# Routing of a mixture of experts, taken apart and placed among the maxima of the first batch

## The chip, the cores and the metric

The kernel runs on one core of a Trainium2 chip. A core has five engines with a queue of instructions each: TensorE (PE in the profile; its weight loads are listed apart as PEld), VectorE (DVE), ScalarE (ACT), GpSimd (POOL) and SyncE (SP, which here only issues DMAs). They run beside each other and wait for each other through semaphores. Each works its own queue off in order. Products of TensorE land in PSUM, everything else lies in SBUF, and DMAs move data between SBUF and the memory outside (DRAM).

The metric is the device time of the whole program in microseconds. Lower is better.

## What is computed

Two layers over `x` of shape (4, 2048, 256), each an attention `s` and a gate `g`, joined as `x + s * silu(g)`. Layer 0 has a windowed attention and an FP8 linear layer. Layer 1, to which the change belongs, has a causal attention with 16 heads of 16 and rotary positions, and a mixture of 8 experts of which each token takes two:

```python
x = x + s0 * silu(ffn0)            # layer 0, on layernorm(x)
xn = layernorm(x)
q, k = rope(xn @ wq.T + bq), rope(xn @ wk.T + bk);  v = xn @ wv.T + bv
att = softmax(where(causal, q @ k.T * 0.25, -inf))
s = (att @ v) @ wo.T + bo
# experts
scores = softmax(xn @ wg);  gates, idx = top_k(scores, 2);  gates /= gates.sum(-1)
m = one_hot(idx) laid out as (2 * T, 8), all first choices before all second ones
loc = ((cumsum(m, 0) - 1) * m).sum(-1)          # place of a choice in its expert
valid = loc < cap;   disp[idx, min(loc, cap - 1)] += xn * valid
out = relu(disp @ w1 + b1) @ w2 + b2
g = sum over the two choices of gates * valid * out[idx, loc]
x = x + s * silu(g)
```

Here T is 8192 tokens and `cap` is 2048, so there are 16384 choices and 16384 slots.

## The kernel before

**Stages.** Layer 0 runs over 16 segments of 512 tokens, in a software pipeline whose steps are written out in a dictionary (`plan`). It also leaves layer 1's normalised rows in DRAM (`xn_d`), their transposes (`xT_d`), the values (`va_d`) and the logits of the experts' choice in SBUF, and it projects q and k of batch 0 (`project`), which go to `qk_d`. Then comes the routing, alone. Then, for each of the four batches, the *maxima* (the largest score of each row and head, over the causal part) and the *attention* (exponentials of the scores less that maximum, and their products with the values). The expert networks are a generator, `experts`, whose pieces are put among the maxima and the attentions of the first three batches and the maxima of the fourth; beside attention `b` the q and k of batch `b + 1` are projected. The last attention has the output projection and the joining of the layers (`finish`) beside it.

**Order.** On TensorE, VectorE, ScalarE and GpSimd the order of the instructions is the order of the program inside `manual_schedule` blocks: layer 0 is one such block, everything from the maxima on is another. What lies between (the routing, L670 to L797, and the first loads) isn't in such a block, and SP's queue isn't ordered by hand either.

**The ring.** `ring` holds four places, each with `qT`, `kT` and `va` of one block of 512 tokens. At the start GpSimd clears all `qT` and sets all `kT` to one (L629, L630), and `fetch` loads a block by four DMAs for q, four for k (128 KB each, L646) and one for the values (L647), all on SP, blocks 0, 1, 2, 3.

**Routing.** `choose` takes the two experts of the last two segments (for the first 14 it has run inside layer 0) into one-hot vectors `oh` and numbers `kmax`. L707 to L726 count the choices ahead of each one: two float32 products with a triangle and with the counts of each partition, masked and summed to `loc`. The rest turns places round: for every slot, which token is in it (`source`). It is a product of two one-hot matrices over 128 columns of choices, in 16 rounds of 8: `at_row` says in which row of a 128 x 128 grid of slots a choice lies, `at_col` in which column, times the token's number plus one. In half of the rounds VectorE makes `at_row` by one comparison (L781), in the others ScalarE by eight squares and one `Relu` (L775, L779). `source` is the list by which GpSimd gathers the experts' rows (L1042).

**Maxima.** `maxima` goes over query blocks `qb` 0 to 3, their four row tiles `r`, four groups of four heads `g`, and the key blocks up to `qb`: 160 score steps a batch. A step is four products into two pair slots of PSUM (`scores`, L830; there are three slots). A full key block is reduced by VectorE straight from PSUM (L898). Of the diagonal one ScalarE copies the square tile out (L902), GpSimd masks it (L912), VectorE reduces the masked tile later (L921) and what lies left of it from PSUM (L905). `whole` (L929) makes the row maximum of all parts; `spread` transposes a block's maxima on TensorE (L937), copies them (L939) and sends them by four DMAs (L941) into spare rows of that block's `qT`, from where the attention's products subtract them. These three are put on a list (`later`) and run some steps on; after the last block seven turns (`TAIL`) empty it.

**Filling.** Before each step `feed` is called with the stall that a planner (`Plan`, with costs of each step) expects on TensorE. It runs pieces of `experts` up to that stall, as long as they aren't 2 us ahead of their share: `IN_M`, 0.209 of all expert work in each batch of maxima, and `IN_A`, 0.055 in each of the first three attentions. In the attention `along` lets the side that is most behind its share step next, and one whose accumulation is open (`held`) before others. The attention goes over query blocks 3, 2, 1, 0.

Of the kernel before, what the change touches and what calls it, by code (L numbers as in the profile page):

```python
# [19 lines left out]
P = 128  # L20
# [24 lines left out]
def d2_kernel(ctx: ExitStack, tc: tile.TileContext, t: dict):  # L45
# [59 lines left out]
    oh = const.tile([P, 2, NT, E], F32, tag="oh", name="oh")  # L105
# [110 lines left out]
    with ExitStack() as l0:  # L216
        w0 = l0.enter_context(tc.tile_pool(name="w0", bufs=1))
        p2 = l0.enter_context(tc.tile_pool(name="l0p2", bufs=2))
        small = l0.enter_context(tc.tile_pool(name="l0small", bufs=4))

# [386 lines left out]
    with tc.tile_pool(name="bvp", bufs=1) as bvp:  # L607
        bvc = bvp.tile([P, 2], F32, tag="bvc", name="bvc")
        nc.scalar.dma_start(out=bvc, in_=t["bv"].rearrange("(c p) -> p c", p=P))
        bvr = bvp.tile([P, 2, P], F32, tag="bvr", name="bvr")  # L610
        nc.scalar.copy(bvr, bc(bvc[:, :, None], [P, 2, P]))
        pb = mm_tile()
        for c in range(2):
            nc.tensor.matmul(
                pb[:, :D], lhsT=bvr[:, c, :], rhs=wo[:, c, :], start=(c == 0), stop=(c == 1)
            )
        nc.vector.tensor_tensor(bo, bo, pb[:, :D], ALU.add)


# [5 lines left out]
    for n in range(NBLK):  # L625
        qT = w1p.tile([P, 4, SEG], F32, tag=f"qT{n}", name=f"qT{n}")
        kT = w1p.tile([P, 4, SEG], F32, tag=f"kT{n}", name=f"kT{n}")
        va = w1p.tile([P, SPT, VW], F32, tag=f"va{n}", name=f"va{n}")
        nc.gpsimd.memset(qT, 0.0)  # L629
        nc.gpsimd.memset(kT, 1.0)  # L630
        ring.append((qT, kT, va))
# [3 lines left out]
    ready = set()  # L635

    def fetch():

        while free and made_qk:
# [3 lines left out]
            for dst, s_ in ((qT, 0), (kT, 1)):  # L643
                src = qk_d[4 * b + i, s_].rearrange("(g j r) n -> j r g n", g=4, j=4)
                for j in range(4):
                    nc.sync.dma_start(out=dst[32 * j : 32 * j + HD, :, :], in_=src[j])  # L646
            nc.sync.dma_start(out=va, in_=va_d[4 * b + i])  # L647
            ready.add((b, i))

    made_qk.extend((0, i) for i in range(4))  # L650
# [21 lines left out]


    with ExitStack() as rt:
        rp = rt.enter_context(tc.tile_pool(name="route", bufs=1))
        KJ = 2 * NT

        def rtile(shape, tag):
            return rp.tile(shape, F32, tag=tag, name=tag)

        tok = rtile([P, NT], "tok")
        nc.gpsimd.iota(
            tok, pattern=[[P, NT]], base=1, channel_multiplier=1,
            allow_small_or_imprecise_dtypes=True,
        )
        along_f = rtile([P, P], "along")
        nc.gpsimd.iota(
            along_f, pattern=[[1, P]], base=0, channel_multiplier=0,
            allow_small_or_imprecise_dtypes=True,
        )  # L690
        ones = rtile([P, P], "ones")
        nc.gpsimd.memset(ones, 1.0)
        tri = rtile([P, P], "tri")
        nc.gpsimd.affine_select(
            out=tri, in_=ones, compare_op=ALU.is_gt, fill=0.0,
            base=0, pattern=[[1, P]], channel_multiplier=-1,
        )

        choose(rp, slice(EARLY * SPT, NT))

        ohf = oh.rearrange("p k t e -> p (k t e)")
        ohj = oh.rearrange("p k t e -> p (k t) e")
        pc = mm_tile()
        for e in range(E):
            nc.tensor.matmul(  # L707
                pc[:, e : e + 1], lhsT=ohj[:, :, e], rhs=ones[:, 0:1], start=True, stop=True
            )
        counts = rtile([P, E], "counts")  # L710
        nc.scalar.copy(counts, pc[:, :E])
        ahead = rtile([P, KJ, E], "ahead")
        nc.vector.tensor_tensor(
# [639 lines left out]
```

## Time and profile before

The three runs shown took 3890.49, 3900.05 and 3896.63 us, a median of 3896.63. The profile is of one execution.

| | us |
|---|---|
| median of three runs | 3896.63 |
| the profiled execution, as timed | 3874.95 |
| its span, first to last instruction | 3873.2 |
| TensorE's last product of layer 0 ends | 482.5 |
| first score of the maxima | 544.2 |
| first expert product | 554.0 |
| batch 0: last score step of blocks 0 and 1 | 663.3 |
| batch 0: first score of the attention | 957.8 |
| first scores of the attention of batches 1, 2, 3 | 1798.6, 2632.2, 3460.2 |

Times inside the profile are from the start of the span. Engines overlap, so busy times don't add up to the span. A releaser (`<-`) is what ended a wait, inferred from semaphores. TensorE's records are modelled at their ends, so a busy TensorE isn't one at its peak. A float32 product appears as two records. The granted clock is a share of full speed.

### The profile page before, as it was taken

What the parts mean: (1) busy time and instruction counts of PE and PEld (TensorE: products, weight loads), DVE (VectorE), ACT (ScalarE), POOL (GpSimd) and SP (SyncE); (2) the same over time, 40 slices, a digit from 0 to 9 for tenths busy, and PEclk for the clock granted to TensorE, in tenths of its full rate; (3) what the DMA queues carried; (4) which work ended last, traced back from release to release, by engine and by line L of the source; (5) the groups of instructions that cost most, each with busy time, mean ns of one, the idle gap of its engine ahead of it and who ended that gap; (6) DMA issues with size and microseconds to landing.
All of it is one profiled execution on the core that took longest, in us unless ns stands there. A gap on an engine that the chain in (4) does not pass through costs nothing.

```text
span 3873.2 us, 53698 instructions
## 1 busy us (share of the span) xinstructions
PE 3672.9 (95%) x21724; PEld 1502.7 (39%) x21724; DVE 2186.5 (56%) x2842; ACT 1773.1 (46%) x2781; POOL 809.4 (21%) x1016
## 2 busy tenths in 40 slices
PE   7999779999999899999999999999999999989998
PEld 3555454444223244443222344443233344433332
DVE  7999768887111258885112278882112478863344
ACT  4665342212666541213666531115666421127775
POOL 4554231110000121110001221110101211013344
PEclk8999889999999999999999999999999999999999
DMA  2444450010120220100022211000112201013232
GB/s 80 143 138 139 167 111 16 30 35 12 33 56 13 75 59 12 46 23 14 31 65 50 58 30 41 16 22 18 53 38 59 53 30 35 12 47 110 89 102 79
DMA packets 131803, 216.86 MB, mean 56 GB/s; under 512 B 18657, under 2 KB 86498, under 8 KB 131554
## 3 DMA queue, kind: packets, MB, share of 16 engines
q1 hardware_dynamic: 116642, 177.21, 15.9%
q0 software_dynamic: 12288, 33.57, 2.9%
q8 instruction: 171, 2.80, 0.3%
q10 hardware_dynamic: 2624, 2.63, 0.2%
q14 instruction: 78, 0.64, 0.1%
HBM read 128.99 MB, written 83.85 MB: 55 GB/s over the span
## 4 chain that ended last, share of the span: by engine, by line
PE 79%; DVE 14%; POOL 2%; DMA 2%; issue 1%; ACT 1%; SPq 0%; POOLq 0%; ACTq 0%; DVEq 0%
PE sp L830 32%; PE so L1006 13%; PE so L1087 13%; PE so L1069 12%; PE so L189 3%; DVE mp L898 3%; DVE rb L203 2%; PE so L955 2%; DVE cm L404 1%; DVE w L406 1%; DVE ra L199 1%; POOL xs L344 1%; POOL xq L346 1%; PE so L1056 1%; DVE mp L921 1%
## 5 line engine op out<-in xcount | busy, mean ns | idle before, releaser
L986 ACT ACTIVATE pt<-sp 128x1024 f32<-128x1024 f32 (+3 forms) x1280 | 1076.6, 893 | 527.2 <-PE sp L830 526.1
L898 DVE TENSOR_REDUCE mp<-sp 128x2 f32<-128x1024 f32 x768 | 904.5, 1220 | 188.3 <-PE sp L830 184.4
L830 PE MATMUL sp<-kT,qT 32*128 32x512 f32 (+3 forms) x5120 | 743.6, 579 | 20.4 <-ACT dg L902 13.1
L830 PE MATMUL sp<-qT,kT 32*128 32x512 f32 (+3 forms) x5120 | 690.8, 583 | 10.0 <-DMA qT<-nT 10.0
L1006 PE MATMUL so<-pt,va 128*32 128x512 f32 (+3 forms) x5120 | 602.7, 543 | 7.5 <-POOL pt L991 6.9
L1087 PE MATMUL so<-w,hT 128*128 128x256 f32 x2048 | 572.5, 404 | 5.2 <-DVE rb L203 4.5
L1069 PE MATMUL so<-xTe,w 128*128 128x512 f32 x1024 | 544.7, 635 | 18.9 <-DVE rb L203 15.2
L902 ACT COPY dg<-sp 128x256 f32<-128x256 f32 x512 | 165.4, 375 | 744.7 <-PE sp L830 712.0
L1087 PEld LDWEIGHTS so<-w,hT 128*128 128x128 f32 x2048 | 350.8, 190 | 358.2 <-issue 312.3
L991 POOL TENSOR_SCALAR_AFFINE_SELECT pt<-pt 128x512 f32<-128x512 f32 x256 | 166.3, 653 | 1236.0 <-ACT pt L986 1130.6
L912 POOL TENSOR_SCALAR_AFFINE_SELECT dg<-dg 128x512 f32<-128x512 f32 x256 | 162.4, 635 | 1249.3 <-ACT dg L902 1243.1
L830 PEld LDWEIGHTS sp<-kT,qT 32*128 32x128 f32 x5120 | 261.6, 185 | 384.0 <-DVE mp L898 142.4
L1075 ACT ACTIVATE hT<-so,b 128x512 f32<-128x512 f32 x256 | 175.9, 687 | 412.9 <-PE so L1069 412.4
L830 PEld LDWEIGHTS sp<-qT,kT 32*128 32x128 f32 x5120 | 225.4, 185 | 291.4 <-issue 203.8
L199 DVE SCALAR_TENSOR_TENSOR ra<-so,bqk,tab 128x512 f32<-128x512 f32 x48 | 36.0, 750 | 480.9 <-PE so L189 480.9
L905 DVE TENSOR_REDUCE mp<-sp 128x2 f32<-128x256 f32 (+2 forms) x384 | 247.4, 687 | 87.7 <-ACT dg L902 86.2
L1069 PEld LDWEIGHTS so<-xTe,w 128*128 128x128 f32 x1024 | 164.8, 190 | 322.2 <-issue 259.3
L1006 PEld LDWEIGHTS so<-pt,va 128*32 128x32 f32 x5120 | 101.4, 108 | 409.5 <-issue 338.2
L1012 DVE STREAM_TRANSPOSE avq<-so 128x512 f32<-128x512 f32 x64 | 45.8, 716 | 365.0 <-PE so L1006 363.4
L921 DVE TENSOR_REDUCE mp<-dg 128x8 f32<-128x1024 f32 x128 | 155.0, 1211 | 28.1 <-POOL dg L912 28.1
L1093 DVE TENSOR_TENSOR ot<-so,b 128x512 f32<-128x512 f32 x64 | 43.7, 683 | 207.2 <-PE so L1087 207.2
L1121 POOL DMA_INDIRECT o<-eout,slot_g x128 | 123.6, 966 | 147.2 <-DVE fz L1149 102.5
(165 smaller groups left out, 2752.4 us busy)
## 6 DMA issues: line engine op xcount, KB each, us to landing
qk_d<-ra SPq DMA_DIRECT2D x128, 128.0 KB
w<-in_w_dram SPq DMA_DIRECT2D x16, 1024.0 KB
eout<-ot SPq DMA_DIRECT2D x32, 512.0 KB
va_d<-vas SPq DMA_DIRECT2D x16, 574.0 KB
va<-va_d SPq DMA_DIRECT2D x16, 574.0 KB
x<-in_x_dram SPq DMA_DIRECT2D x16, 512.0 KB
tab<-in_rope_dram SPq DMA_DIRECT2D x16, 512.0 KB
rec<-rec_d SPq DMA_DIRECT2D x32, 256.0 KB
```

The costliest lines, as they stand in the source:

```text
L830: nc.tensor.matmul(pairs[j // 2][:, j % 2, :w], lhsT=lhsT[r0 : r0 + 32], rhs=rhs[r0 : r0 + 32], start=True, stop=True,)
L898: nc.vector.tensor_reduce(mp[:, h0 : h0 + 2, kc], sp, AX.X, ALU.max)
L902: nc.scalar.copy(dg[:, d0 : d0 + 2, :], sp[:, :, r * P : w])
L905: nc.vector.tensor_reduce(mp[:, h0 : h0 + 2, qb + 1], sp[:, :, : r * P], AX.X, ALU.max)
L912: nc.gpsimd.affine_select(out=dg[:, d0 : d0 + 4, :], in_=dg[:, d0 : d0 + 4, :], compare_op=ALU.is_ge, fill=NEG, base=0, pattern=[[0, 4], [ ...
L921: nc.vector.tensor_reduce(mp[:, 4 * g - 4 : 4 * g + 4, qb], dg, AX.X, ALU.max)
L986: nc.scalar.activation(pt[:, 2 * p : 2 * p + 2, c0:], sp[:, :, : SEG - c0], AF.Exp, scale=SCALE)
L991: nc.gpsimd.affine_select(out=pt[:, :, c0 : c0 + P], in_=pt[:, :, c0 : c0 + P], compare_op=ALU.is_ge, fill=0.0, base=0, pattern=[[0, 4], [ ...
L1006: nc.tensor.matmul(av[32 * j : 32 * j + 32, c0:], lhsT=va[:, kt % 4, h0 : h0 + 32], rhs=pt[:, j, c0:], start=(kt == 0), stop=last,)
L1069: nc.tensor.matmul(ph, lhsT=w1[:, c, hc * P : (hc + 1) * P], rhs=xT[:, c, :], start=(c == 0), stop=(c == 1),)
L1075: nc.scalar.activation(hT[:, hc, :], ph, AF.Relu, bias=b1[:, hc : hc + 1])
L1087: nc.tensor.matmul(po[:, u * D : (u + 1) * D], lhsT=hT[:, hc, a * P : (a + 1) * P], rhs=w2[:, hc, :], start=(hc == 0), stop=(hc == 7),)
```

## The change

It does these things at once:

- The routing becomes a generator, `route`, in the hand-ordered part. `feed` runs one piece of it at each score step of batch 0 as long as there are any, and no expert piece meanwhile. It ends at the 44th call. The next call issues the first gather of the experts, and expert pieces follow when the planner's TensorE time is 8 us further.
- Whole numbers that bfloat16 holds exactly are kept in it: `oh`, the triangle, the counts ahead, `in_e`, `at_col`, `at_row`. A token's number no longer fits, so it is split: `oh1` carries its row plus one, `oh2` its tile, and `at_col` has two halves, one made by VectorE and one by GpSimd. One product of 256 columns makes both sums; `first_` and `src` join them. All sixteen `at_row` are made by ScalarE. `in_e` is made a round at a time.
- The product of `bv` with `wo` that completes `bo` is the routing's last piece.
- Blocks 1 and 0 are loaded first, q on SP's queue, k on ScalarE's, the values after; then blocks 3 and 2 on SP. VectorE clears `qT`, GpSimd still sets `kT`.
- In the maxima the rows of blocks 1 and 0 alternate, then come block 3 and block 2. The last block's `spread` is returned and becomes a piece (`due`) of the attention that follows, or runs ahead of the last attention.
- The list `later` is emptied by as many turns as it needs, with less expert work in each. Batch 0 has a share of 0.186 of the experts, the others 0.216.
- The pools of layer 0 are opened in another order; the row maxima have a pool of their own; `avq` and `yq` have one buffer.

The core of the diff, with unchanged pieces of moved code left out:

```diff
-    oh = const.tile([P, 2, NT, E], F32, tag="oh", name="oh")
+    oh = const.tile([P, 2, NT, E], BF16, tag="oh", name="oh")
...
-        w0 = l0.enter_context(tc.tile_pool(name="w0", bufs=1))
         p2 = l0.enter_context(tc.tile_pool(name="l0p2", bufs=2))
         small = l0.enter_context(tc.tile_pool(name="l0small", bufs=4))
+        w0 = l0.enter_context(tc.tile_pool(name="w0", bufs=1))
...
-        nc.gpsimd.memset(qT, 0.0)
+        nc.vector.memset(qT, 0.0)
...
-    def fetch():
+    def fetch(queues=(nc.sync, nc.sync)):
+        later = []
         while free and made_qk:
...
-            for dst, s_ in ((qT, 0), (kT, 1)):
+            for dst, s_, queue in ((qT, 0, queues[0]), (kT, 1, queues[1])):
...
-                    nc.sync.dma_start(out=dst[32 * j : 32 * j + HD, :, :], in_=src[j])
-            nc.sync.dma_start(out=va, in_=va_d[4 * b + i])
+                    queue.dma_start(out=dst[32 * j : 32 * j + HD, :, :], in_=src[j])
+            later.append((va, va_d[4 * b + i]))
+        for va, src in later:
+            nc.sync.dma_start(out=va, in_=src)
...
-    made_qk.extend((0, i) for i in range(4))
+    made_qk.extend(((0, 1), (0, 0)))
+    fetch((nc.sync, nc.scalar))
+    made_qk.extend(((0, 3), (0, 2)))
     fetch()
...
+    def route(rp):
...
+        choose(rp, slice(EARLY * SPT, NT))
+        plan2.on("DVE", 5.0)
+        yield 0
...
+        oh1 = rtile([P, 2, NT, E], "oh1", BF16)
+        nc.vector.tensor_scalar(oh1, oh, row1, None, ALU.mult)
+        oh2 = rtile([P, 2, NT, E], "oh2", BF16)
+        nc.vector.tensor_tensor(
+            oh2, oh, bc(along_f[:, None, :NT, None], [P, 2, NT, E]), ALU.mult
+        )
...
+        def build(n):
+            js = slice(n * NB, (n + 1) * NB)
+            in_e = rtile([P, NB, CT], "in_e", BF16, 2)
+            nc.vector.tensor_tensor(
+                in_e, bc(along_f[:, None, :CT], [P, NB, CT]),
+                bc(rowcol[:, 1, js, None], [P, NB, CT]), ALU.is_equal,
+            )
+            at_col = rtile([P, NB, 2, P], "at_col", BF16, 2)
+            for i, (engine, o) in enumerate(((nc.vector, oh1), (nc.gpsimd, oh2))):
+                engine.tensor_tensor(
+                    at_col[:, :, i, :].rearrange("p j (e c) -> p j e c", c=CT),
+                    bc(o.rearrange("p k t e -> p (k t) e")[:, js, :, None], [P, NB, E, CT]),
+                    bc(in_e[:, :, None, :], [P, NB, E, CT]), ALU.mult,
+                )
+            plan2.on("DVE", 1.6)
+            at_row = rtile([P, NB, P], "at_row", BF16, 3)
+            for u in range(NB):
+                nc.scalar.activation(
+                    at_row[:, u, :], along_f, AF.Square,
+                    bias=minus_row[:, n * NB + u : n * NB + u + 1],
+                )
+            nc.scalar.activation(at_row, at_row, AF.Relu, scale=-1.0, bias=one)
+            plan2.on("ACT", 3.1)
+            made[n] = at_row, at_col
+
+        for n in range(NJ + 1):
+            if n < NJ:
+                build(n)
+                yield 0
+            if n > 0:
+                at_row, at_col = made.pop(n - 1)
+                for u in range(NB):
+                    j = (n - 1) * NB + u
+                    nc.tensor.matmul(
+                        ps[:, : 2 * P], lhsT=at_row[:, u, :],
+                        rhs=at_col[:, u, :, :].rearrange("p i c -> p (i c)"),
+                        start=(j == 0), stop=(j == KJ - 1),
+                    )
+                yield 0.9
...
-        for qb in range(4):
+        rows_ = [(q, r) for r in range(SPT) for q in (1, 0)]
+        rows_ += [(q, r) for q in (3, 2) for r in range(SPT)]
+        nms, last = {}, None
+        for qb, r in rows_:
...
-            later.append((3, spread))
-        for _ in range(TAIL):
+            if (qb, r) == rows_[-1]:
+                last = spread
+            else:
+                later.append((3, spread))
+        while later:
             turn()
-            feed(2.0, 1.0)
+            feed(1.0, 1.0)
+        return last
...
+    def one_piece(f):
+        f()
+        yield 0.58
...
-    IN_M = (1.0 - (B - 1) * IN_A) / B
+    IN_M = [0.186] + [(1.0 - 0.186 - (B - 1) * IN_A) / (B - 1)] * (B - 1)
...
-            exp.step()
+            began = None
             def feed(us, share):
+                nonlocal began
+                if not rt.over:
+                    rt.step()
+                    return
+                if began is None:
+                    exp.step()
+                    began = plan2.t["PE"]
+                if plan2.t["PE"] < began + 8.0:
+                    return
...
-                    maxima(mp_, b, feed)
+                    if b == 0:
+                        rt = Side(route(rs.enter_context(tc.tile_pool(name="route", bufs=1))), 0.0)
+                    spread = maxima(mp_, b, feed)
+                    rt.drain()
+                due.queue.append(one_piece(spread))
                 if b + 1 == B:
+                    exp.close()
+                    due.drain()
                     break
```

## The prediction

> **What bounds the kernel now.** I read the page first (busy shares, the row of slices), then the busy times by stretch, the chain of waits, the groups of each stretch, and last the timeline at the places that the change touches.
>
> ```profile
> PE 3672.9 (95%) x21724; PEld 1502.7 (39%) x21724; DVE 2186.5 (56%) x2842; ACT 1773.1 (46%) x2781; POOL 809.4 (21%) x1016
> ...
> PE   7999779999999899999999999999999999989998
> ```
>
> TensorE is busy nearly everywhere, so time is TensorE's work plus its idle time, and a change pays by the idle time it removes. The slices hide where that lies; the stretches show it (columns: PE, weight load, DVE, ACT, POOL, each with its count, then clock, DMA share, GB/s):
>
> ```profile
> 482.50:554.00 71.50, 47.43 (x308) 40.64 (x309) 42.91 (x64) 31.74 (x82) 19.61 (x18) 0.80 0.78 146
> 544.00:663.30 119.30, 113.20 (x578) 51.63 (x578) 86.92 (x106) 34.37 (x85) 31.85 (x44) 0.97 0.06 19
> 663.30:957.80 294.50, 287.52 (x1418) 130.01 (x1418) 245.38 (x245) 55.29 (x117) 39.26 (x52) 0.99 0.08 26
> ```
>
> The first is the routing: TensorE's last product of layer 0 ends at 482.5, its first score starts at 544.2, the first expert product at 554.0. The second holds batch 0's maxima of query blocks 0 and 1, the third those of 2 and 3. In both, experts fill TensorE.
>
> **The routing's price, and what replaces it.** The groups between 482 and 544 us (busy, mean ns | idle before):
>
> ```profile
> L766 DVE TENSOR_TENSOR at_col<-ahead,in_e 128x1024 f32<-128x1024 f32 x16 | 19.4, 1222 | 2.6 <-PE mm L787 2.4
> ...
> L775 ACT ACTIVATE at_row<-along,minus_row 128x128 f32<-128x128 f32 x64 | 19.6, 388 | 16.5 <-DVE minus_row L749 10.9 <-PE mm L787 5.5
> L779 ACT ACTIVATE at_row<-at_row,ones 128x1024 f32<-128x1024 f32 x8 | 9.2, 1148 | 0.3
> ...
> L787 PE MATMUL mm<-at_col,at_row 128*128 128x128 f32 x256 | 31.4, 286 | 10.0 <-DVE at_col L766 9.4 <-ACT at_row L779 0.2
> ```
>
> The change deletes this stretch and gives the same work to the 48 score steps of blocks 1 and 0, one piece a step, with no expert before the pieces end (step 44) and 8 us of planned TensorE time more, so until about step 48. What counts is when those 48 steps end. Before, that was at 663.3, with expert work done beside them:
>
> ```profile
> L1069 PE MATMUL so<-xTe,w 128*128 128x512 f32 x64 | 35.1, 645 | 0.2 <-ACT xTe L1059 0.2
> ...
> L1087 PE MATMUL so<-w,hT 128*128 128x256 f32 x110 | 29.6, 398 | 0.0
> ```
>
> A float32 product has two records here and takes 0.95 us (four records in 1.91 of the chain) and 0.48 us: 32 x 0.95 + 55 x 0.48 + 2.2 for transposes = 59 us of experts, about 62 with some 3 us of alternation. They must be done later, at full price. So the new kernel breaks even here if its 48 steps end at 663.3 - 62 = **601 us**.
>
> VectorE's share of the 48 steps, from the same groups: 32 full maxima in pairs of 2.36 us (37.8), 16 diagonal ones of 1.21 (19.4), the left parts 6.0 + 10.3 + 14.6, eight row maxima (1.5): 89.6 us. Routing on VectorE, start to start: choosing 4.2 (483.8 to 488.0), `ahead` 1.1, `spot` 1.3, `loc` 1.1, the casts 0.8, `oh1` and `oh2` 1.5, sixteen blocks of `in_e` (0.2) and `at_col` (1.15) 21.5, the tail 2.3: 33.9 us. ScalarE now makes all sixteen `at_row`: 2.45 + 1.15 = 3.6 us each, 57.6, beside 32 x 0.65 = 20.8 of diagonal copies: 78 us, less than VectorE's 123.5. Per piece pair it is 4.25 against at least 5.1 in block 1, and 4.9 against 4.2 only in row 1 of block 0. TensorE's 128 products shrink below the old 0.24 us each and lie in idle time: no charge, nor would 31 us bind.
>
> When can they start? First places: eight loads of 128 KB for block 1's q and k, then eight for block 0's. The loads of before ran at this rate:
>
> ```profile
> 504.00:508.00 4.00, 0.00 (x0) 0.00 (x0) 3.93 (x12) 1.27 (x5) 0.00 (x0) 0.54 1.09 127
> ```
>
> The DMA engines are full (1.09) at 127 GB/s, 1.05 us a load; a second issuing queue can't add to that. From about 483 (SP is behind the `va_d` store issued at 482.9, ScalarE's queue behind its last copy) q1 and k1 take 8.4 us, with 2 us of landing to 493; the second step also wants k of block 0, 8.4 us later, at 502. If SP takes its loads ahead of that store (`qT`'s clearing moves to VectorE, idle from 475.4), it is 5 us less. I take 500; choosing (4.2) runs before that. VectorE then has 123.5 - 4.2 = 119.3 us: 619 without gaps.
>
> Gaps: three pair slots, two per step. In each of block 1's sixteen head groups the full step needs a slot that the diagonal's left maximum frees, so VectorE waits one score step (1.07) less the second left maximum (0.38 to 0.91), or for a diagonal maximum queued between: 0.5 us each, 8 us. At the clock of a half-idle TensorE (0.50 between 488 and 500) a step takes 1 us more: 24. I take 16, nearer the middle since TensorE will be some 45% busy. The end: **635 us**, 34 late.
>
> [...]
>
> ```profile
> 487.57 1.80 POOL L630 MEMSET kT<- 128x2048 f32 x1
> ...
> 488.02 1.43 DVE L728 TENSOR_SCALAR base<-kmax 128x128 f32<-128x128 f32 x1
> ```
>
> L728 took 1.43 us instead of the 0.23 of its kind and ended just after the memset on POOL. [...]
>
> **The seams.** Before, block 3 is last in the maxima and first in attention:
>
> ```profile
> 954.63 0.23 DVE L929 TENSOR_REDUCE nm<-mp 128x16 f32<-128x80 f32 x1
> 954.92 0.09 PEld L937 LDWEIGHTS so<-ident,nm 128*16 128x16 f32 x1 [2.51 <-DVE nm L929]
> 954.92 0.38 PE L937 MATMUL so<-ident,nm 128*16 128x128 f32 x1 [2.22 <-DVE nm L929]
> ...
> 957.78 0.51 PEld L830 LDWEIGHTS sp<-qT,kT 32*128 32x128 f32 x8 [2.77 <-DMA qT<-nT]
> 957.78 2.09 PE L830 MATMUL sp<-qT,kT 32*128 32x512 f32 x8 [2.47 <-DMA qT<-nT]
> 959.80 0.50 PEld L189 LDWEIGHTS so<-xT,wqk 128*128 128x128 f32 x2 [1.50 <-issue]
> ```
>
> TensorE waits for the last row maximum, ScalarE's copy and the DMA into `qT`, then runs slowly (2.09 for a step of 1.07). From 952.0 to 963.1 it does 3.7 us of work: 7.3 lost; 8.5, 7.2 and 12.8 at the other seams. With block 2 last, attention starts on a finished block, and block 2's transposes are a piece of attention; its DMA has the sixteen-item-a-group sweep of block 3 for cover. What is late next is a free pair slot and the same row maximum, 2 us, and the output's own load of `fy` at the last seam (3.6 us). I take 5 us a seam, 20 in all; bounds 3 (the DMA wait without the slow restart) and 6.5. The tail's expert feeds move; they are work either way.
>
> **Edits at nothing.** `bv`'s product (2.0 us) goes into idle TensorE time. Single `avq` and `yq` are written and read by VectorE alone, in order. The exchanged pools only change what the clearing waits for. The experts' share of 0.186 instead of 0.209 puts 23 us into later stages, all TensorE-bound: moved, not saved. SP gains no transfers; ScalarE issues eight loads, some 4 us at the 0.43 of `wo`'s, before its first copy is due. POOL's gathers come at step 45, under the 8 us hold.
>
> **Sum**, against the profiled execution (span 3873.2, 3874.95 as timed): +34 - 20 = **+14 us**, 3887. The three runs shown have a median of 3896.63, 22 above it; the difference is carried over: 3911 us, 0.36% slower. A measurement here can tell about 0.3%, 11.7 us, from no change.
>
> **Rivals.**
> 1. *No gaps on VectorE* (not slower). In the 48 steps its queue runs dense from the first load at 491: the loads get ahead of the store and queued maxima cover every slot wait. 491 + 119.3 = 610, +9 - 20 = -11: 3886. For it: VectorE was dense at 508 to 512. Against: layer 0's 0.50 clock after any pause. It decides if the 48th step ends before 609; at 621 the two kernels tie.
> [...]
> 3. *The seam wait changes its name*: the row maximum and the slots cost what the DMA did, gain 4 instead of 20: +30, 3927. For it: L937's 2.2 us precede the DMA.
> That the routing isn't hidden at all is excluded: its steps share the engines with scores that had to run anyway.
>
> **Numbers.** My forecast 0.42 (own range 3897 to 3924), rival 1 0.26, rival 2 0.12, rival 3 0.20. Low end: rival 1 with bfloat16 at double rate, 3877. High end: rival 2 with 3 us a seam, near 3957; cut to 3952. Faster by more than 0.3%: half of rival 1, and 0.07 for gains that I don't see, 0.20. Within 0.3%: the rest of rival 1 and a third of my forecast, 0.27. Slower: 0.53.
>
> **What would show it.** The first score near 493 and the second held by k of block 0; the 48th step near 635 and the first expert product there; VectorE over 80% busy from 500 to 635, TensorE near 45%; `at_col` at 1.2 us on VectorE, POOL's lengthened; no wait on `qT<-nT` at the seams, and 2 us on `nm` or a slot. A 48th step before 609, or seams that gain 10 us each, would make me wrong downward; `at_col` over 2 us on VectorE upward.

## The result, and the profile after

Five runs of each kernel on one chip: the changed one took 3915.97 us in the median (3909.48 to 3917.59), the kernel before 3896.63 (3890.49 to 3900.05). The ratio is 1.0048, 95% interval 1.0035 to 1.0061: 19 us slower. The forecast was 3911, 14 us slower.

The profiled execution after took 3917.59, near its median, the one before 3874.95, 22 below its own. So the 42.6 us between the two profiles (span 3915.8 against 3873.2) are not the change alone, as the controls below show. From the page, the busy times and the rows of slices:

```profile
PE 3693.1 (94%) x21584; PEld 1494.5 (38%) x21584; DVE 2187.3 (56%) x2855; ACT 1801.1 (46%) x2854; POOL 848.9 (22%) x1029
...
PE   7999668999999999999999999999999999989998
...
PEclk8999856999999999999999999999999999999999
```

The hole that the routing left in TensorE's row isn't filled: the three slices from 392 to 685 us hold 6, 6 and 8 tenths where they held 7, 7 and 9. In the row of the granted clock the same slices have 8, 5 and 6 tenths (8, 8 and 9 before). The stretches, with the same columns as before:

```profile
483.90:503.20 19.30, 0.02 (x1) 0.00 (x1) 7.36 (x6) 0.44 (x2) 7.80 (x9) 0.63 0.93 183
503.20:668.80 165.60, 134.09 (x528) 60.15 (x529) 120.11 (x170) 75.96 (x210) 69.74 (x51) 0.57 0.21 42
668.80:976.00 307.20, 304.03 (x1516) 140.32 (x1514) 245.89 (x246) 62.81 (x129) 43.79 (x57) 0.99 0.09 27
```

First a pause for the loads; then the 48 score steps with the routing, which end at 668.8; then the rest of batch 0's maxima. The forecast counted from the second step on, which here begins at 511.8:

```profile
511.80:668.80 157.00, 132.44 (x520) 59.02 (x521) 116.83 (x155) 75.16 (x207) 69.10 (x50) 0.58 0.17 37
```

VectorE works 116.8 us there, near the predicted 119.3, but in 157.0 us, not in 135. Groups of the first two stretches (a *full maximum*, L948, reduces a full key block; a *left maximum*, L955, what lies left of the diagonal):

```profile
L696 PE MATMUL sp<-kT,qT 32*128 32x512 f32 x192 | 65.3, 1027 | 14.2 <-DVE mp L955 7.9 <-DMA kT<-qk_d 4.7 <-ACT dg L952 0.9
...
L845 ACT ACTIVATE at_row<-along,minus_row 128x128 bf16<-128x128 f32 x128 | 39.2, 397 | 0.0
L948 DVE TENSOR_REDUCE mp<-sp 128x2 f32<-128x1024 f32 x32 | 37.7, 1221 | 21.9 <-PE sp L696 21.9
L861 PE MATMUL so<-at_col,at_row 128*128 128x256 bf16 x128 | 28.5, 399 | 0.1
...
L836 DVE TENSOR_TENSOR at_col<-oh,in_e 128x1024 bf16<-128x1024 bf16 x16 | 20.2, 1264 | 0.6
...
L849 ACT ACTIVATE at_row<-at_row,one 128x1024 bf16<-128x1024 bf16 x16 | 18.4, 1149 | 0.6
```

The durations on VectorE and ScalarE are the predicted ones. What stands out is VectorE's idle time ahead of the full maxima, 21.9 us waiting for scores (15.8 more lie ahead of the left maxima), and the scores' own length: 1027 ns a record, where the rest of batch 0 has 643.

Why the first steps came late (SPq and ACTq are DMA issues):

```profile
484.85 1.26 SPq L638 DMA_DIRECT2D va<-va_d  x2
487.15 23.39 SPq L635 DMA_DIRECT2D qT<-qk_d  x12
...
486.92 17.36 ACTq L635 DMA_DIRECT2D kT<-qk_d  x8
507.21 0.65 ACT L952 COPY dg<-sp 128x256 f32<-128x256 f32 x2 [22.81 <-DMA qT<-qk_d]
507.75 0.27 ACT L125 ACTIVATE sm<-sm 128x64 f32<-128x64 f32 x1
...
503.23 0.76 PE L696 MATMUL sp<-kT,qT 32*128 32x128 f32 x2 [19.31 <-DMA qT<-qk_d]
506.24 0.89 PE L696 MATMUL sp<-kT,qT 32*128 32x128 f32 x6 [2.25 <-DMA qT<-qk_d]
511.83 3.04 PE L696 MATMUL sp<-kT,qT 32*128 32x512 f32 x8 [4.70 <-DMA kT<-qk_d]
```

SP's queue isn't ordered by hand, and it took two loads of `va` (574 KB each) ahead of q. Then it issued q of three blocks, not of two, while ScalarE issued k. The first step began at 503.2 and the second at 511.8. ScalarE was occupied with issuing for 17.4 us, until 504.3. But the exponential of `choose` (L125) ran at 507.75 because it stands behind the first step's copy (L952), and that waited for q.

The order of SP's loads could be seen in the profile before:

```profile
485.78 0.80 SPq L647 DMA_DIRECT2D va<-va_d  x2
487.66 1.75 SPq L646 DMA_DIRECT2D qT<-qk_d  x4
```

The seam of batch 0:

```profile
974.04 1.99 PE L1143 MATMUL so<-w,hT 128*128 128x256 f32 x8
...
975.97 1.14 PE L696 MATMUL sp<-qT,kT 32*128 32x512 f32 x8
...
977.97 0.22 DVE L979 TENSOR_REDUCE nm<-mp 128x16 f32<-128x64 f32 x1
```

The attention's first scores follow the experts at once and take 1.14 us a step instead of 2.09, before the last row maximum is even made.

### The profile page after: what moved, and what is told of

The parts are those of the page before. It is cut to its first block, busy times and chain, and to the rows that moved or that the text cites. A ratio compares the mean times of both kernels' runs of the same rounds, so it can differ in the third digit from the quotient of the medians.

```text
span 3915.8 us, 53494 instructions
## 1 busy us (share of the span) xinstructions
PE 3693.1 (94%) x21584; PEld 1494.5 (38%) x21584; DVE 2187.3 (56%) x2855; ACT 1801.1 (46%) x2854; POOL 848.9 (22%) x1029
## 4 chain that ended last, share of the span: by engine, by line
PE 80%; DVE 13%; DMA 2%; POOL 2%; issue 1%; ACT 1%; SPq 0%; another core or an unknown queue 0%; POOLq 0%; ACTq 0%; DVEq 0%
PE sp L696 32%; PE so L1143 13%; PE so L1062 13%; PE so L1125 12%; PE so L190 3%; DVE mp L948 2%; DVE rb L204 2%; PE so L1011 2%; DVE cm L406 1%; DVE w L408 1%; DVE ra L200 1%; PE so L1112 1%; POOL xs L346 1%; PE so L861 1%; POOL xq L348 1%
## 5 line engine op out<-in xcount | busy, mean ns | idle before, releaser
L948 DVE TENSOR_REDUCE mp<-sp 128x2 f32<-128x1024 f32 x768 | 904.6, 1221 | 239.2 <-PE sp L696 232.4
L696 PE MATMUL sp<-kT,qT 32*128 32x512 f32 (+3 forms) x5120 | 771.8, 600 | 68.1 <-DMA qT<-qk_d 21.6
L952 ACT COPY dg<-sp 128x256 f32<-128x256 f32 x512 | 165.6, 375 | 761.6 <-PE sp L696 700.2
L955 DVE TENSOR_REDUCE mp<-sp 128x2 f32<-128x256 f32 (+2 forms) x384 | 247.4, 687 | 94.9 <-ACT dg L952 91.1
L1098 POOL DMA_INDIRECT xd<-xn_d,source x128 | 121.8, 951 | 144.6 <-PE so L1112 105.9
```

The costliest lines, as they stand in the source:

```text
L696: nc.tensor.matmul(pairs[j // 2][:, j % 2, :w], lhsT=lhsT[r0 : r0 + 32], rhs=rhs[r0 : r0 + 32], start=True, stop=True,)
L948: nc.vector.tensor_reduce(mp[:, h0 : h0 + 2, kc], sp, AX.X, ALU.max)
L952: nc.scalar.copy(dg[:, d0 : d0 + 2, :], sp[:, :, r * P : w])
L955: nc.vector.tensor_reduce(mp[:, h0 : h0 + 2, qb + 1], sp[:, :, : r * P], AX.X, ALU.max)
```

## The experiments

Times differ by chip, so each kernel is compared by its ratio to the kernel before on its own chip. That kernel took 3876 to 3878 us where eleven of these twelve ran, and 3902.55 for the last. Where two medians are compared below, both are from chips on which it took 3876 to 3878.

**1. Both kernels again, profiled on one chip.**

> The kernel before, unchanged, profiled once more. Its profiled execution was 22 us under the median of its runs, and the last attention of the changed kernel looked 18.8 us longer than in that profile. If this is chance of one execution, this profile shows a span near 3890 to 3900 and a last attention (from its first score to the end) some 10 to 18 us longer than 413.0, with the 48 score steps of blocks 0 and 1 still ending near 663. If it is a cost of the change, the last attention here is 413 again. Time: equal to the kernel before within 0.3%.

> The changed kernel, unchanged, once more, so that its profile and time stand beside those of the kernel before on one chip. The kernel before took 3876.24 us here and 3896.63 where the changed kernel was first profiled, so part of the 42.6 us between the two first profiles is between chips. Expected: a ratio of 1.0048 again (3895), a span near 3894, and a last attention of some 417 us instead of the 431.8 of the first profile. If that 431.8 belongs to the change, it stays.

Before: 3876.03, span 3875.5. Changed: 3899.42, ratio 1.0056 (1.0043 to 1.0070). The two spans differ by 22.1 us, and the changed kernel's last attention takes 417.1 us, against 413.1. The 431.8 of its first profile didn't come back here; 437.6 came in the last experiment, where the kernel before is slower too. The ratio isn't larger there, so the change is hardly its cause; but the kernel before was never profiled where it is slower. Starts of the stages:

| | before | changed | difference |
|---|---|---|---|
| first score | 546.5 | 501.7 | -44.8 |
| 48th step ends | 664.3 | 664.5 | 0.2 |
| attention, batch 0 | 960.1 | 972.0 | 11.9 |
| maxima, batch 1 | 1386.7 | 1394.8 | 8.1 |
| attention, batch 2 | 2634.5 | 2649.6 | 15.1 |
| attention, batch 3 | 3462.4 | 3480.5 | 18.1 |
| end | 3875.5 | 3897.6 | 22.1 |

The 48 steps end level, but without the 57 us of experts that lay beside them before. Those are paid for from there on, less what the seams gain.

**2. The seams alone, and the change without them.** The first is the kernel before with the change's `maxima`, `due` and single buffers. The second:

```diff
-        rows_ += [(q, r) for q in (3, 2) for r in range(SPT)]
+        rows_ += [(q, r) for q in (2, 3) for r in range(SPT)]
+        if b > 0:
+            rows_ = [(q, r) for q in range(4) for r in range(SPT)]
...
-            if (qb, r) == rows_[-1]:
-                last = spread
-            else:
-                later.append((3, spread))
+            later.append((3, spread))
```

> The kernel before with its routing as it was, alone and in float32, and only the order of the maxima changed: rows of blocks 1 and 0 in turn, then block 3, then block 2, whose spread is a piece of the attention that follows. If the seams gain what was predicted (5 us each), 20 us less than before: about 3877. If they gain the 7 us that the changed kernel's profile suggests at the first three seams and nothing at the last, about 3875. If the wait only changes its name (rival 3), 4 us less: 3893. In all cases the routing's stretch is untouched: first score near 544, and the first score of the attention of batch 0 follows the maxima without the wait for the DMA into qT.

> The changed kernel with the seams put back: block 3 is last in the maxima, its spread is on the list, and seven turns empty it; routing among the maxima as changed (blocks 1 and 0 in turn in batch 0). If seams and routing add up, this one is slower than the changed kernel by what the seams-only kernel gains over the kernel before: 3936 at 20 us. Then the routing alone costs about 40 us against the kernel before: not the 66 us by which its 48 steps end too late, so that experts done later must cost some 25 us less than their full price; and close to the predicted +34 in sum only because two terms were wrong in opposite directions.

Seams alone: 3862.08, ratio 0.9967 (0.9956 to 0.9979): 13 us gained, not 20. By spans of maxima and attention together, the seams of batches 0 to 3 gain 2.0, 5.6, 6.1 and 0.2 us. The last one's wait does change its name, as in the changed kernel (profile of the control):

```profile
3480.19 0.38 PE L989 MATMUL so<-ident,nm 128*16 128x128 f32 x1 [3.82 <-DVE nm L979]
3480.50 2.09 PE L696 MATMUL sp<-qT,kT 32*128 32x512 f32 x8
3489.36 1.19 PE L1011 MATMUL so<-wo,fy 128*128 128x256 f32 x2 [6.77 <-DMA fy<-yT_d]
```

There `spread` runs ahead of the attention, so the row maximum is waited for, and `fy` after it. Change without seams: 3906.86, ratio 1.0079 (1.0065 to 1.0092): the routing by itself costs some 31 us, near the predicted 34. Had seams and routing added up, it would have taken 3912 (the expectation, with seams of 20 us, was 3936). So on top of the routing the seams gain only 7 us, not 13, though these intervals allow either. In the profiles the first three gain 1.6, 7.1 and 5.0 there and the last loses 6.3.

**3. Experts held back, routing untouched.** On the seams-only kernel, with batch 0's share at 0.186:

```diff
             def feed(us, share):
+                calls[0] += 1
+                if calls[0] <= 48:
+                    return
```

> The seams-only kernel (routing alone and in float32, as before) with no expert piece beside the first 48 score steps of batch 0, and batch 0's share of the experts 0.186 as in the changed kernel: it measures by itself what experts cost that are done later. They are 56.6 us of TensorE work. Their 48 steps (VectorE 87 us) should take 95 to 105 us instead of 119, so end 15 to 24 us sooner. If deferred experts cost their full price, the kernel is 33 to 42 us slower than the seams-only one (3862): 3895 to 3904. If they cost the 0.68 of it that the stages of the late-va kernel suggest (38.5 us), 15 to 24 us slower: 3877 to 3886.

It took 3912.19, ratio 1.0090: 50 us more than the seams-only kernel, outside every expectation. Both halves of the answer are in the profile. The 48 steps, seams-only kernel first:

```profile
544.90:663.90 119.00, 111.66 (x566) 50.62 (x568) 84.39 (x103) 33.16 (x82) 31.31 (x43) 0.97 0.06 18
```

```profile
544.00:675.00 131.00, 105.24 (x382) 43.77 (x382) 83.05 (x100) 20.04 (x62) 23.67 (x35) 0.52 0.02 5
```

With less work on TensorE the same steps take longer: 133.0 us from the first score to the end of the 48th step instead of 119.8. VectorE's work in them is the same (84 us), while the granted clock falls from 0.97 to 0.52 and the scores occupy TensorE for 107.2 us instead of 53.4. The experts hadn't only filled gaps; they had kept TensorE fast. That the clock is the cause is tried from the other side in experiment 5. From the end of the 48th step (664.7 and 676.9) to the end of the program the two kernels need 3195.3 and 3233.6 us: 38.3 us more for 57 us of experts, two thirds of full price. The changed kernel needs 3233.1. Of the 38 us, 29 lie in the maxima, which took on some 55 us of expert products (an estimate from their number, at 0.95 and 0.48 us each): half price. The other 9 lie in the attentions. That of batch 1 alone is 10 us longer, with fewer expert products than before; its projection waits 7.7 us for loads of `xT` there instead of 1.2. The other half of the price shows in the scores of the rest of batch 0, kernel before and changed kernel:

```profile
L830 PE MATMUL sp<-kT,qT 32*128 32x512 f32 x710 | 112.6, 639 | 0.7 <-DVE mp L898 0.5
```

```profile
L696 PE MATMUL sp<-kT,qT 32*128 32x512 f32 x708 | 104.9, 647 | 0.6 <-DVE mp L955 0.6
```

The same scores keep TensorE busy for 7.7 us less where more experts lie between them. A reading of this, which no run tests: part of its busy time before was waiting for pair slots, hidden by the modelled ends of matmuls.

**4. The first loads.** The va loads and the first expert weights are held until the routing's ninth piece; the second kernel also puts k on SP:

```diff
+        while hold:
+            va, va_src = hold.pop(0)
+            nc.gpsimd.memset(va[:, 0, 0:1], 0.0)
+            nc.sync.dma_start(out=va, in_=va_src)
...
-    fetch((nc.sync, nc.scalar))
+    fetch((nc.sync, None))
```

> The changed kernel with the four loads of va and the first experts' weights held until the routing's ninth piece (a one-element write on GpSimd into each tile stands ahead of its load), so that q of block 1 is the first large load on SP; k stays on ScalarE's queue. Two va loads (574 KB each, about 9 us of the DMA engines at 127 GB/s) went ahead of q. If the DMA engines set the start, the first score comes 8 to 9 us sooner (494), the second step near 503, the 48th near 660, and the kernel is some 6 to 9 us faster: 3908. If the issuing of k on ScalarE's queue (17.4 us for eight) sets it, the second step stays within 2 us of 511.8 and the time within 3 us of 3916. New one-element writes cost under 1 us.

> As the kernel with the late va loads, with k of blocks 1 and 0 issued on SP as well, q1, k1, q0, k0 in turn; nothing but layer 0's weights is issued by ScalarE there. Against the changed kernel: if ScalarE's issuing (17.4 us for eight) sets the second step and holds up choosing, then choosing's exponential runs near 490 instead of 507.8, the second step comes near 503, and the 48th step 5 to 9 us before that of the late-va kernel (658): 650; 5 to 9 us less time than that one. If the DMA engines' rate sets it (1.05 us a load), the second step is at 503 to 505 for either queue, and only choosing moves, 4 us. If one queue issues slower than two, the second step is later than 506.

Late va: first score 497.0, 48th step 659.3, ratio 1.0051 (1.0037 to 1.0065), against 501.7, 664.5 and 1.0056. Five microseconds sooner in the profile, not separable in the time. One queue: first score 500.0, second step at 508.3, 48th at 665.4, ratio 1.0053 (1.0039 to 1.0067). The third expectation came, a second step later than 506. Of the 6 us between the two kernels' 48th steps, 2.6 were there when layer 0 ended; the rest doesn't show in the time. A second queue brought no rate here: from 490 to 508 the DMA engines were full with either (a share of 1.08, 131 GB/s with one queue, 133 with two). Issuing cost ScalarE 17.4 us for eight loads in the changed kernel's first profile. It held up nothing that was ready: without it, with one queue, the exponential of `choose` still ran right behind the first step's copy (502.20, the copy at 501.67).

**5. The clock.** Products on bfloat16 tiles that belong to no computation, into a PSUM bank of their own: 96 of them, then some 230, from before the first score on:

```diff
+            for _ in range(4):
+                nc.tensor.matmul(rt_fill[0], lhsT=tri, rhs=ohf[:, :512], start=True, stop=True)
```

> The changed kernel with 96 bfloat16 products of 512 columns that belong to no computation (four ahead of each building piece, two behind each of the eight-product pieces, into a PSUM bank of their own), to keep TensorE busier while the routing runs. The 48 steps took 162 to 164 us with VectorE busy 120.1 and a granted clock of 0.57; score records there are 2.1 times as long as in the kernel before (110 us against 51). If the low clock makes the gaps, the clock rises above 0.8, score records shrink towards 55 us, and the 48th step comes 15 to 25 us sooner (near 645), the kernel 15 to 25 us faster: 3873 to 3880. If the gaps come from VectorE's order and the three pair slots alone, the 48th step stays within 5 us and so does the time. If the products don't raise the clock, they add up to 40 us of TensorE time to a TensorE that is busy 134 of 166: 10 to 20 us slower.

> As the kernel with 96 idle products, but with 48 of them ahead of the first score (in the pause of the loads), six at each early piece, five at each building piece and four at each eight-product piece, some 230 in all, on a constant tile, none part of the computation. With 96 of them the granted clock of the 48 steps rose from about 0.6 to 0.72, 0.91 and 0.78 in its three parts, and the 48 steps fell from 161 to 152 us. If the clock is the cause of the gaps, it is above 0.85 throughout here, score records (108 us with the change, 85 with 96 products) come to 60 to 70, the 48 steps take 138 to 145 us, and the kernel is 5 to 12 us faster than with 96: 3877 to 3884. If the rest of the gaps belongs to VectorE's order and the slots, it stays at 150 to 154, or gets longer because TensorE is then full: 3886 to 3895.

With 96: 3888.40, ratio 1.0031 (1.0021 to 1.0042), 11 us faster than the changed kernel, between the first two expectations; the 48 steps end at 654.9. With 230: 3894.22, ratio 1.0042 (1.0028 to 1.0056), end 660.7, as expected if the clock isn't all. The stretch from 560 to 600 us in the control, with 96, and with 230:

```profile
560.00:600.00 40.00, 34.20 (x148) 16.43 (x144) 30.16 (x42) 25.46 (x71) 21.96 (x15) 0.59 0.00 1
```

```profile
560.00:600.00 40.00, 35.52 (x191) 15.55 (x194) 33.59 (x47) 29.02 (x81) 23.48 (x15) 0.91 0.00 1
```

```profile
560.00:600.00 40.00, 37.69 (x223) 17.09 (x221) 33.07 (x48) 29.36 (x81) 24.99 (x16) 1.00 0.00 1
```

At 0.59 VectorE works 30.2 of 40 us, at 0.91 33.6, at full clock 33.1. So the clock is a part of the gaps, not all. Why 230 do worse than 96 wasn't tried; they take more of TensorE's time (133.7 us in the 48 steps against 127.1), in which scores can't run.

**6. The pieces' place.** The control's timeline of one head group of block 1, in the second row of query tiles:

```profile
556.12 0.28 DVE L830 TENSOR_TENSOR in_e<-along,rowcol 128x128 bf16<-128x128 f32 x1
...
556.28 1.89 PE L861 MATMUL so<-at_col,at_row 128*128 128x256 bf16 x8
...
556.43 1.23 DVE L836 TENSOR_TENSOR at_col<-oh,in_e 128x1024 bf16<-128x1024 bf16 x1
...
557.58 0.75 DVE L955 TENSOR_REDUCE mp<-sp 128x2 f32<-128x256 f32 x2
558.10 0.52 PEld L696 LDWEIGHTS sp<-kT,qT 32*128 32x128 f32 x8 [0.41 <-DVE mp L955]
558.10 2.68 PE L696 MATMUL sp<-kT,qT 32*128 32x512 f32 x12
...
560.26 2.36 DVE L948 TENSOR_REDUCE mp<-sp 128x2 f32<-128x1024 f32 x2 [1.93 <-PE sp L696]
```

The diagonal step's left maximum (L955) frees the slot that TensorE needs next (`<-DVE mp L955`). It stands behind `in_e` and `at_col`, and after it VectorE has only full maxima left, whose scores TensorE is then only beginning: idle for 1.93 us. One empty piece more shifts the building by one step, between the left maximum and the full ones:

```diff
         plan2.on("DVE", 2.0)
         yield 0
+        yield 0
```

> The changed kernel with one empty piece more ahead of the sixteen rounds, so that each building piece (1.5 us of VectorE) stands in the order between a head group's diagonal step and its full step instead of ahead of the diagonal one, and the eight products ahead of the diagonal step. In the changed kernel VectorE waits 19.0 us between 511 and 658 for the full step's scores (32 maxima) and 15.8 us ahead of the diagonal steps' left maxima; a row of the timeline shows VectorE's left maximum, then the full scores at 2.1 us with VectorE idle for 1.9. If the place of the pieces in VectorE's order makes the gap, the wait ahead of the full maxima falls from 19.0 to 10 or less, the 48 steps from 161 to 148 to 153 us, and the kernel takes 8 to 13 us less than the changed one: a ratio of 1.0020 to 1.0030. If the wait only moves to the diagonal step, whose cover is then gone, the sum of the two waits stays near 35 and the ratio at 1.0048 to 1.0056.

It took 3909.72 against 3902.55 for the kernel before: ratio 1.0015 (1.0006 to 1.0024), so two thirds of the loss are gone, more than was expected. In the shifted kernel the building covers the wait:

```profile
555.19 0.75 DVE L956 TENSOR_REDUCE mp<-sp 128x2 f32<-128x256 f32 x2
...
555.85 0.28 DVE L831 TENSOR_TENSOR in_e<-along,rowcol 128x128 bf16<-128x128 f32 x1
556.16 1.23 DVE L837 TENSOR_TENSOR at_col<-oh,in_e 128x1024 bf16<-128x1024 bf16 x1
...
557.31 2.35 DVE L949 TENSOR_REDUCE mp<-sp 128x2 f32<-128x1024 f32 x2
```

Between 511 and 658 us (control) and 511 and 646 (shifted), all 32 full maxima and the idle time ahead of them:

```profile
L948 DVE TENSOR_REDUCE mp<-sp 128x2 f32<-128x1024 f32 x32 | 37.7, 1221 | 19.0 <-PE sp L696 19.0
```

```profile
L949 DVE TENSOR_REDUCE mp<-sp 128x2 f32<-128x1024 f32 x32 | 37.7, 1220 | 6.2 <-PE sp L696 5.7
```

The waits ahead of the left maxima stay near 15 us. From 560 to 600 VectorE works 33.1 us here at a clock of 0.60, as much as with 230 idle products at full clock. The 48 steps in all four kernels:

| | us | granted clock | VectorE busy | TensorE busy |
|---|---|---|---|---|
| changed (control) | 162.8 | 0.62 | 120.0 | 127.6 |
| with 96 idle products | 153.7 | 0.80 | 120.1 | 127.1 |
| with some 230 | 157.0 | 0.88 | 120.0 | 133.7 |
| shifted | 149.7 | 0.66 | 120.6 | 121.5 |

The clock of the shifted kernel is a little higher too, so a small part of its gain may be the clock's.

**7. What can be had from it.** The seams-only kernel with the last seam made like the others (row maxima in a pool that outlives the experts, the final part's products from 3% of the attention on), and then with the counting in bfloat16 and `bv`'s product behind the routing:

```diff
-                    exp.close()
-                    due.drain()
+                    exp.close()
...
-        along(attend(at, B - 1, project_out), ATT_T, [(due, 0.0, 0.0), (fin, 0.0, 1.0)])
+        fin.step()
+        along(attend(at, B - 1, project_out), ATT_T, [(due, 0.0, 0.0), (fin, -0.03, 1.0)])
```

and for the second

```diff
-        ones = rtile([P, P], "ones")
+        ones = rtile([P, P], "ones", BF16)
...
-        tri = rtile([P, P], "tri")
+        tri = rtile([P, P], "tri", BF16)
...
-        ahead = rtile([P, KJ, E], "ahead")
+        ahead = rtile([P, KJ, E], "ahead", BF16)
```

> The seams-only kernel with the last seam treated as the other three: block 2's spread is a piece of the last attention too (its row maxima have a pool that outlives the experts), and the final part's first matrix products start 3% into the attention, behind their loads. In the seams-only kernel this seam still lost 3.8 us for the last row maximum and 6.8 us for the load of fy. If those waits are the seam, 6 to 10 us less than the seams-only kernel's 3862: 3852 to 3856. If something else is late right behind them, within 3 us of 3862.

> The kernel with the last seam treated, and two parts of the change taken over into a routing that stays alone in its place: one-hot vectors, triangle, ones and the counts ahead in bfloat16 (their products take one pass), and the product of bv with wo moved behind the routing. The two-hot product stays in float32. In the kernel before, the eight counting products took 3.8 us, the four products of the counts ahead 6.9, and the product of bv waited for its weights until 492.5, 2.2 us after the one-hot vectors were there, and took 2.0. Expected: the counting in 0.7 us and the counts in about 2.5, so first score 8 to 11 us sooner than 546 and 8 to 11 us less time than the kernel with the last seam treated: 3842 to 3848. If the loop of sixteen rounds waits for the loads or for GpSimd's clearing, 0 to 3 us less.

Last seam: 3864.04, ratio 0.9966, no different from the seams alone, though the last maxima and attention are 3.7 us shorter in the profile. With the counting in bfloat16: 3860.59, ratio 0.9957 (0.9943 to 0.9971), the lowest of all, 17 us under the kernel before; but its intervals overlap the seams-only kernel's, and the expected 8 to 11 us more didn't come. In bfloat16 the eight counting products took 0.66 us in eight records, as float32 in the kernel before 3.76 us in 16. The two-hot products begin at 507.9 instead of 515.3 in the last-seam kernel. Then `bv`'s product, now in front of the first score, gives most of it back: it waits 3.7 us for the copy of a bias that is loaded only then, and takes 2.1 (first score 546.6, against 548.0). And VectorE's small operations met GpSimd's clearing:

```profile
495.25 0.23 DVE L725 TENSOR_SCALAR valid<-loc 128x128 f32<-128x128 f32 x1
495.39 1.91 DVE L727 CAST loc_i<-loc 128x128 int32<-128x128 f32 x1
...
497.34 1.79 DVE L728 TENSOR_SCALAR loc<-loc 128x128 f32<-128x128 f32 x1
...
495.33 1.90 POOL L619 MEMSET qT<- 128x2048 f32 x1
497.17 1.87 POOL L620 MEMSET kT<- 128x2048 f32 x1
```

## Why the prediction was right, and where it was not

The direction and the size (19 us, forecast 14) hold. Of the two parts of the sum the routing's +34 holds (+31 alone, +37 on top of the seams); the seams' -20 is too much (-13 alone, -7 on top of the routing). Inside the first part two terms were wrong by much, in opposite directions, so that it came out is luck.

- **VectorE's work, 119.3 us after choosing.** Right: 116.8 from the second step on, 120.1 with choosing (predicted 123.5). `at_col` took 1264 ns in bfloat16 against 1222 in float32, so bfloat16 brought it nothing. The low end of the range, 3877, has bfloat16 at a double rate; no run shows that for VectorE.
- **Second step at 500.** It came at 511.8 (510.2 in the control). The DMA rate was right (127 GB/s taken, 131 to 133 in experiment 4); what it was multiplied by was not: two va loads and q of a third block shared the engines with the sixteen loads counted. Without the va loads ahead (experiment 4) the second step began at 502.5, half of it at 505.6. The remark that SP might take its loads ahead of the store had the right question, its free order, and missed what else could go ahead, though the profile before shows va ahead of q. "Some 4 us" for ScalarE's eight issues were 17.4. "Choosing runs before that" was wrong: it ran from 508.1 to 512.1, since its exponential stands behind the first step's copy. It hardly cost anything, since VectorE waited for the second step's scores until 514.9.
- **Gaps of 16 us, bounds 8 to 24.** This term failed. From the second step to 668.8 there are 157.0 us for 116.8 of work: 40 us. Two causes were shown: the place of the building pieces in VectorE's order (shifting them brought 13 to 16 us, by ratios on different chips) and the clock (11 us with 96 idle products). Whether the two add up wasn't tried, and what makes the rest stays open. The step that went wrong is "I take 16, nearer the middle since TensorE will be some 45% busy": TensorE's records covered 134 of 165.6 us and the clock was still 0.57. And the gap was priced as a slot wait of half a microsecond a head group, where one is near 1.2 (19.0 over sixteen in the control) at the full maxima alone, with 15.8 us more ahead of the left ones. The end of the 48 steps was therefore 34 us later than predicted (668.8 against 635).
- **TensorE's 128 products, no charge.** 28.5 us of busy time, hardly less than the 31.4 of the float32 ones, since they ran mostly at the low clock (0.57 in the 48 steps; 1.89 us for eight in the timeline of experiment 6). In that timeline they lie in idle time, as taken: they end at 558.2, as the next slot comes free. No run leaves them out.
- **Experts done later, 62 us "at full price".** They cost 38 (experiment 3). The break-even end is then not 601 but near 626 (664.3 less 38.3), and the control's 664.5 is 38 late: nearly the predicted 34, of two errors of some 30 and 25 us that cancel. The premise behind it, that a stage whose TensorE is 98% busy has no room, was wrong. (The 663.3 that it starts from is where the 49th step begins; the 48th ends at 662.0 in that profile.)
- **Seams, 5 us each.** Right for two (5.6 and 6.2), mis-sized for batch 0 (2.0), and the last gained 0.2: there the third rival held, a new wait in place of the old one.
- **The rivals.** VectorE dense (end 610): no. Rival 2's chance of 0.12 and the high end of the range count on VectorE's half of `at_col` losing time to GpSimd's; no run shows that term. The runs show the reverse: GpSimd's half took 1.90 us in the one block of the control where VectorE's half had ended before, and 2.85 to 2.94 in the fifteen where the two overlapped by about 1.1; VectorE's stayed at 1.22 to 1.23 in fourteen of these. So GpSimd's half was the one that got longer, by about one microsecond. L728, which the prediction shows at 1.43 us, is another pair: its row has one input (`base<-kmax`), and the memset beside it none (`kT<-`).
- **The offset of 22 us** between the profile before and the median fits the difference between chips: that profile's 3874.95 is what the kernel takes on the chips of the controls (3876). On which chip it was taken isn't on record.

## What to carry to other kernels

Before taking filler away from TensorE, ask what clock the remaining work will get: 57 us of experts kept the 48 steps at 0.97, and without them the same steps were 13 us longer, at 0.52. When work is put between the steps of another loop, its place within a step counts as much as its amount: it belongs where the engine would otherwise wait for the step's product, not ahead of the operation that frees the next buffer (here 149.7 us for the 48 steps against 162.8). And a stage with TensorE 98% busy by modelled records can still have room: the maxima here took on 55 us of products for 29.

## What was not expected of the hardware

- The granted clock was 0.57 over the 165.6 us from 503.2 to 668.8, in which TensorE's records covered 81% of the time, and in the 40 us at 0.59 they covered 34.2. In the kernel with the experts held back it was 0.50 from 549 to 681 us without a break, with records over 108 of 132 us and no gap between them longer than 1.4. So it stayed down there without a longer pause, unless the modelled ends hide one. What share of work would raise it, no run here shows.
- Small casts and `tensor_scalar` operations on VectorE took 1.8 to 1.9 us in the last kernel of experiment 7, each about as long as the clearing on GpSimd beside it, while others of the same size (L725) took 0.23. In the kernel before, where they came after GpSimd's clearing had ended (499.9), the same casts and `tensor_scalar` operations took 0.22 to 0.29. Why, no run here shows.
- The kernel before took 3896.63 us where the changed kernel was first timed and 3902.55 where the shifted one was, 19 to 27 more than on the three chips of the other runs. Where it was slower, the last attention of the changed kernel and of the shifted one was 15 and 20 us longer than the changed kernel's on the faster chip (431.8 and 437.6 against 417.1); the changed kernel's other stages differed by 3 us or less.
